# A prologue with its own step table: how the first groups of a graph-network kernel are started

## The chip, the cores and the metric

The kernel runs on one core of one Trainium2 chip. The metric is the device time of one execution in microseconds (us). The program is one instruction stream per engine (TensorE, written PE; VectorE, DVE; ScalarE, ACT; GpSimd, POOL) and the queue of SyncE (SP), which issues DMAs. Times inside an execution are counted from the start of its span.

## The reference

There are 128 independent graphs of 128 nodes with 256 features, and a weighted adjacency matrix for each. Two layers follow one another, all in float32:

```
h = relu(layernorm(x));  x1 = x + adj @ (h @ W0) + b0
h2 = relu(layernorm(x1))
p_h = h2 @ fc_w[:, head h] + fc_b        # 8 heads of 256
logits_h[n, m] = (p_h q_w)[n] + (p_h k_w)[m] + (1 - adj[n, m]) * (-1e9)
attn_h = softmax(leaky_relu(logits_h, 0.01))
out = x1 + sigmoid(concat_h(attn_h @ p_h) @ fp_w + fp_b + h2)
```

## The kernel before, in words

Work is done in 32 groups of 4 graphs. `s0`, `s1`, `s2`, ... are the groups; group g goes through several phases, and the main loop for group g also carries earlier phases of the groups g+1 to g+4. A pair is two graphs of a group, and a unit is one pair with four of its eight heads, so that a group has 4 units.

The weights of a head are folded: `setup_weights` (L208) multiplies a head's fc_w with its part of fp_w, so that the large product per head is attn @ h2 (`aggregate`, L562, tile g_ps) and then times the folded weights (`multiply`, L600, tile acc). Each 2x2 block product is done with seven products in place of eight; `take` (L573) forms their left sides f0 to f6 from g_ps on ACT, DVE and POOL, `setup_sums` (L272) forms the sums of weights, and `combine` (L618) puts the products together.

The vector that gives q and k is folded as well: `setup_wqk` (L184) makes fc_w times q_w and k_w, one product of two columns per head and half, into wqk_p. `setup_bias` makes the constant part. `setup_fb` (L244) and `setup_fb2` (L251) form fc_b times fp_w: twelve of sixteen chunks one after the other on DVE, four on POOL; `setup_fpb` (L260) sums over partitions on PE.

For a group the attention runs as: `make_qk` (L449) and `turn_qk` (L464) produce q and k; k is written to DRAM (k_mem) and read back spread over partitions by `load_k` (tile kq). `masked` (L495) spreads k with a DVE transpose and adds the mask; `leaky` (L508), eight ACT instructions for a graph; `head_max` (L516) on DVE; `exps` (L524), eight ACT instructions with sums; `normal` (L532) divides on POOL after a DVE reciprocal. The attention must then be transposed. `move` (L540) does it with 16 DMAs of 32-row blocks for a pair on the SP queue, and `turn` (L551) with a DVE transpose inside the blocks for each graph. The normalised h2 of the next groups is transposed in the same manner by `move_h2` (16 DMAs) and `turn_h2_blocks`, and in the prologue by `turn_h2` (PE transposes and ACT copies). `turn_blocks` and `turn_adj` are the same two ways for the adjacency.

The order on every engine is written by hand: under `manual_schedule` each engine executes the instructions in the order in which the program issues them, and waits at its head for what its instruction needs. A straight prologue prepares s0 and s1 and part of s2. Then the loop goes through the groups, each in 44 slots (four units of 11 entries); a slot has one PE step, and the table PLAN attaches other steps to it (slot, which group, function). For the first group a table FIRST_PLAN adds the steps which would otherwise belong to an earlier group, and the steps in `LATE` are left out of PLAN. All PSUM tiles but acc come from one pool of six.

```
    ORDER = [("g", 0, 0), 3, 0, ("g", 1, 1), 1, 4, ("g", 1, 0), 6, 5, ("g", 0, 1), 2]
    ps_m = ctx.enter_context(tc.tile_pool(name="ps_m", bufs=6, space=PSUM))
            if g == 0:
                for at_, f, *args in FIRST_PLAN:
            for at_, who, f, *args in PLAN:
                if at_ != slot or (g == 0 and f in LATE):
```

Of the kernel before, what the change touches and what calls it, by code (L numbers as in the profile page):

```python
# [9 lines left out]
FP = mybir.dt.float32  # L10
# [5 lines left out]
P = 128  # L16
D = 256
NC = D // P
H = 8
# [9 lines left out]
def gnn_then_gat_kernel(  # L29
# [109 lines left out]
    mk = sp.tile([P, 1], FP, name="mk")  # L139
    ones = sp.tile([P, P], FP, name="ones")  # L140
# [6 lines left out]
    def setup_rows():  # L147
# [3 lines left out]
        nc.vector.tensor_copy(cols, cp)  # L151
        for two in range(2):
# [31 lines left out]
    def setup_wqk(c):  # L184

        qk_cols = cols[:, NK:ROWS].rearrange("p (two c) -> p c two", two=2)
        wp = ps_m.tile([P, H, 2], FP, name="wp", tag="m")
        for h in range(H):
            for kk in range(NC):
                nc.tensor.matmul(  # L190
                    wp[:, h, :],
                    lhsT=fcwT[:, NC * h + kk, ts(c, P)],
                    rhs=qk_cols[:, kk, :],
                    start=(kk == 0),
                    stop=(kk == NC - 1),
                )
        nc.vector.tensor_copy(
            wqk_p[:, c, 0 : 2 * H].rearrange("p (two h) -> p two h", two=2),
            wp.rearrange("p h two -> p two h"),
        )  # L200

    def setup_wqk_order():
        for j in range(NB):
            for c in range(NC):
                n = 2 * (j % 2) + c
                nc.vector.tensor_copy(wqk[ts(j, Q), c], wqk_p[ts(n, Q), j // 2])
# [31 lines left out]


    NV = NK - 4  # L240
    fb = sp.tile([P, D], FP, name="fb")
    fb2 = sp.tile([P, NK - NV, D], FP, name="fb2")

    def setup_fb(k):  # L244
        col = cols[:, k : k + 1]
        if k == 0:
            nc.vector.tensor_scalar(fb, fpw[:, k], col, None, ALU.mult)
        else:
            nc.vector.scalar_tensor_tensor(fb, fpw[:, k], col, fb, ALU.mult, ALU.add)

    def setup_fb2():  # L251
        n = NK - NV
        nc.gpsimd.tensor_tensor(
            fb2, fpw[:, NV:NK], cols[:, NV:NK].unsqueeze(2).to_broadcast([P, n, D]), ALU.mult
        )
        while n > 1:
            n //= 2
            nc.gpsimd.tensor_tensor(fb2[:, 0:n], fb2[:, 0:n], fb2[:, n : 2 * n], ALU.add)
# [226 lines left out]

    def spread(s, b):

        if b % 2 == 0:
            s["a", b // 2] = at.tile([P, NB, 2, H, Q], FP, name="attn", tag="attn", bufs=3)
        nc.vector.transpose(  # L490
            s["a", b // 2][:, :, b % 2],
            s["kq"][:, :, b].unsqueeze(3).to_broadcast([P, NB, H, Q]),
        )

    def masked(s, b):  # L495
        spread(s, b)
        a = s["a", b // 2][:, :, b % 2]
# [10 lines left out]
    def leaky(s, b, h0=0, nh=H):  # L508
        a = s["a", b // 2][:, :, b % 2]
# [6 lines left out]
    def head_max(s, b):  # L516
        a = s["a", b // 2][:, :, b % 2]
# [6 lines left out]
    def exps(s, b, h0, nh):  # L524
        a = s["a", b // 2][:, :, b % 2]
# [6 lines left out]
    def normal(s, b):  # L532
        a = s["a", b // 2][:, :, b % 2]
# [6 lines left out]
    def move(s, pair, blocks=range(NB * NB), queues=(nc.sync,)):  # L540
# [4 lines left out]
        for n in blocks:  # L545
            i, j = divmod(n, NB)
            queues[n % len(queues)].dma_start(  # L547
                s["ab", pair][ts(j, Q), i], s["a", pair][ts(i, Q), j]
            )

    def turn(s, b):  # L551
# [4 lines left out]
        )  # L556

# [203 lines left out]
    LATE = (shift_both, n2_apply, move_h2, turn_h2_blocks, make_qk, turn_qk, load_k, turn)  # L761
# [39 lines left out]
    n2_apply(s0, 1)  # L801
    for half in range(2):
        n1_stats(s1, half)
    scale((s1, "n1"), root=True)
    setup_bias()
    begin(s2)
    setup_fb2()
    for k in range(NV):
        setup_fb(k)
    setup_wqk(0)  # L810
    turn_h2(s0, 0)
    turn_h2(s0, 1)
    setup_wqk(1)
    make_qk(s0, wqk_p)
    turn_qk(s0)
    load_k(s0)
    for half in range(2):
        n1_apply(s1, half)
    turn_adj(s1)
    make_mask(s1)  # L820
    add_b0(s1)
    for half in range(2):
        n1_stats(s2, half)
    first_a(s1, 0)
    first_a(s1, 1)
    masked(s0, 0)
    leaky(s0, 0)
    masked(s0, 1)
    leaky(s0, 1)
    first_b(s1, 0)  # L830
    first_b(s1, 1)
    head_max(s0, 0)
    exps(s0, 0, 0, H)
    head_max(s0, 1)
    exps(s0, 1, 0, H)
    setup_weights(0, 0, True)
    normal(s0, 0)
    n2_stats(s1, 0)
    setup_weights(0, 1, True)
    n2_stats(s1, 1)  # L840
    setup_weights(1, 0, True)
    scale((s1, "n2"), (s2, "n1"))
    normal(s0, 1)
    setup_weights(1, 1, True)
    for half in range(2):
        n2_apply(s1, half)
    for h in range(2, 4):
        setup_weights(h, 0, True)
        setup_weights(h, 1, True)
    turn_h2(s1, 0)  # L850
    turn_h2(s1, 1)
    move(s0, 0, queues=(nc.sync, nc.sync, nc.scalar))
    setup_weights(4, 0, True)
    setup_weights(4, 1, True)
    make_qk(s1, wqk_p)
    setup_wqk_order()
    masked(s0, 2)
    for h in range(5, H):
        setup_weights(h, 0, False)
        setup_weights(h, 1, False)  # L860
    leaky(s0, 2)
    masked(s0, 3)
    leaky(s0, 3)
    turn_qk(s1)
    load_k(s1)
    turn(s0, 0)
    turn(s0, 1)
    head_max(s0, 2)
    setup_fpb()
    setup_sums(0)  # L870
    exps(s0, 2, 0, H)
    setup.close()
    pool["un"] = ctx.enter_context(tc.tile_pool(name="unit", bufs=2))
    FIRST_PLAN = [
        (0, load_blocks, s2),
        (1, begin, s3),
        (1, turn_blocks, s2),
        (1, normal, s0, 2),
        (1, head_max, s0, 3),
        (1, n1_apply, s2, 0),  # L880
        (1, n1_apply, s2, 1),
        (2, exps, s0, 3, 0, H),
        (2, add_b0, s2),
        (6, normal, s0, 3),
        (6, move, s0, 1),
# [25 lines left out]
    for g in range(NG):  # L911
# [4 lines left out]
        for slot in range(4 * len(ORDER)):  # L916
# [6 lines left out]
            if g == 0:  # L923
                for at_, f, *args in FIRST_PLAN:
                    if at_ == slot:
                        f(*args)
# [53 lines left out]
```

## Time and profile before

| what | value |
|---|---|
| time, median of 3 runs | 1558.01 us (1555.54 to 1558.44) |
| profiled execution, its own time | 1552.82 us |
| span of that execution | 1550.9 us |
| PE busy | 1494.5 us (96%) |
| DVE busy | 1312.8 us (85%) |
| ACT busy | 1098.5 us (71%) |
| POOL busy | 938.3 us (61%) |
| mean granted TensorE clock | 0.982 |

A share of busy time is a mean over the whole span, and the stretch before the loop has other limits than the loop. The views by stretch, by waits and by time are therefore the ones to read. A line such as "L610 PE MATMUL acc<-wts,f" names a source line, the engine, the operation, the tile written and those read.

### The profile page before, as it was taken

How to read it: one execution, taken by the hardware profiler on the slowest of the kernel's cores; microseconds unless marked ns; L12 is line 12 of the kernel's file. 1: busy time of each engine (PE TensorE's matmuls, PEld its weight loads, DVE VectorE, ACT ScalarE, POOL GpSimd, SP SyncE). 2: the span in 40 equal slices, each digit the busy share in tenths (PEclk: the TensorE clock that was granted, in tenths of full speed). 3: DMA queues.
4: the chain of work that ended last, by engine and by line, in shares of the span. 5: the costliest groups of instructions: out<-in, count | busy, mean ns of one | idle time of the engine just before them, and what ended most of it. 6: DMA issues, size and time to landing. Idle time of an engine off the chain costs nothing.

```text
span 1550.9 us, 30658 instructions
## 1 busy us (share of the span) xinstructions
PE 1494.5 (96%) x9953; PEld 1209.9 (78%) x9953; DVE 1312.8 (85%) x2286; ACT 1098.5 (71%) x3830; POOL 938.3 (61%) x692
## 2 busy tenths in 40 slices
PE   7777999999999999999999999999999999999998
PEld 7655787888888878788878888877788887788786
DVE  5676888998888899888889988888998888898763
ACT  3683788767778867677877777787677778777651
POOL 3154665666666656676656667665566766566563
PEclk8889999999999999999999999999999999999999
DMA  5142444434444443444444344444434444433320
GB/s 184 31 90 64 92 96 96 97 81 104 106 91 99 95 95 83 101 107 85 98 96 98 83 103 100 93 99 96 94 85 104 98 96 97 97 79 82 74 69 27
DMA packets 259688, 142.07 MB, mean 92 GB/s; under 512 B 174900, under 2 KB 226504, under 8 KB 259272
## 3 DMA queue, kind: packets, MB, share of 16 engines
q1 hardware_dynamic: 259288, 139.79, 40.4%
q8 instruction: 78, 1.28, 0.4%
q14 instruction: 82, 0.67, 0.2%
q10 hardware_dynamic: 240, 0.33, 0.1%
HBM read 39.86 MB, written 17.30 MB: 37 GB/s over the span
## 4 chain that ended last, share of the span: by engine, by line
ACT 33%; DVE 31%; SPq 11%; PE 9%; issue 6%; DMA 6%; POOL 3%; DVEq 0%; ACTq 0%; POOLq 0%
ACT attn L527 14%; ACT attn L511 11%; SPq L547 9%; DVE attn L498 7%; DVE attn L490 5%; PE acc L610 4%; ACT h L320 4%; DMA attnB<-attn 4%; DVE st L286 4%; DVE attnT L554 3%; DVE f L586 2%; DVE x L391 2%; PE g_ps L565 2%; DVE f L587 2%; POOL attn L536 2%
## 5 line engine op out<-in xcount | busy, mean ns | idle before, releaser
L610 PEld LDWEIGHTS acc<-wts,f 128*128 128x128 f32 x7168 | 888.3, 192 | 260.4 <-issue 180.4
L610 PE MATMUL acc<-wts,f 128*128 128x128 f32 x7168 | 894.8, 275 | 15.7 <-DVE z L626 15.6
L565 PE MATMUL g_ps<-attnT,h 128*128 128x512 f32 x1024 | 530.6, 600 | 5.7 <-DVE attnT L554 3.8
L527 ACT ACTIVATE attn<-attn,nmax 128x128 f32<-128x128 f32 x1024 | 397.5, 397 | 0.0
L588 POOL TENSOR_TENSOR f<-f,f 128x512 f32<-128x512 f32 x128 | 163.4, 1277 | 356.3 <-DVE f L586 356.2
L511 ACT ACTIVATE attn<-attn,q 128x128 f32<-128x128 f32 x1024 | 313.0, 392 | 42.0 <-DVE attn L498 22.1
L536 POOL TENSOR_TENSOR attn<-attn,total 128x1024 f32<-128x1024 f32 x128 | 245.3, 1916 | 113.1 <-DVE total L535 98.7
L590 ACT COPY f<-g_ps 128x512 f32<-128x512 f32 x128 | 73.8, 576 | 267.6 <-PE g_ps L565 267.6
L591 POOL TENSOR_TENSOR f<-f,f 128x512 f32<-128x512 f32 x128 | 209.3, 1635 | 7.8 <-ACT f L590 5.2
L527 ACT ACTIVATION_READ_ACCUMULATOR attn<-attn,nmax 128x1 f32 x1024 | 201.3, 197 | 0.0
L498 DVE TENSOR_TENSOR attn<-attn,mask 128x1024 f32<-128x1024 f32 x128 | 186.4, 1456 | 4.5
L519 DVE TENSOR_REDUCE nmax<-attn 128x8 f32<-128x1024 f32 x128 | 153.9, 1203 | 23.4 <-ACT attn L511 23.3
L490 DVE STREAM_TRANSPOSE attn<-kq 128x1024 f32<-128x1024 f32 x128 | 157.1, 1228 | 14.8 <-DMA kq<-k_mem 14.8
L565 PEld LDWEIGHTS g_ps<-attnT,h 128*128 128x128 f32 x1024 | 156.6, 193 | 14.0 <-issue 9.8
L554 DVE STREAM_TRANSPOSE attnT<-attnB 128x1024 f32<-128x1024 f32 x128 | 153.1, 1215 | 9.7 <-DMA attnB<-attn 6.2
L586 DVE TENSOR_TENSOR f<-g_ps,f 128x512 f32<-128x512 f32 x128 | 87.0, 680 | 50.8 <-issue 24.5
L384 PE MATMUL x_ps<-w_sb,ahT 128*128 128x256 f32 x512 | 122.5, 383 | 0.0
L654 POOL TENSOR_TENSOR z<-z,h 128x256 f32<-128x256 f32 x128 | 90.7, 730 | 40.5 <-DVE z L626 39.9
L384 PEld LDWEIGHTS x_ps<-w_sb,ahT 128*128 128x128 f32 x512 | 94.1, 193 | 11.4 <-issue 0.5
L582 ACT COPY f<-g_ps 128x512 f32<-128x512 f32 x128 | 74.4, 581 | 40.2 <-PE g_ps L565 40.2
L664 DVE SCALAR_TENSOR_TENSOR z<-z,x 128x1024 f32<-128x1024 f32 (+1 forms) x33 | 90.1, 2730 | 7.9 <-ACT z L660 7.9
L587 DVE TENSOR_TENSOR f<-f,g_ps 128x512 f32<-128x512 f32 x128 | 86.4, 675 | 0.0
(93 smaller groups left out, 1282.3 us busy)
## 6 DMA issues: line engine op xcount, KB each, us to landing
attnB<-attn SPq DMA_DIRECT2D x1019, 64.0 KB, 2.0
xg<-in_x_dram SPq DMA_DIRECT2D x32, 512.0 KB, 4.0
out_dram<-z SPq DMA_DIRECT2D x31, 512.0 KB, 3.1
h2B<-h SPq DMA_DIRECT2D x480, 32.0 KB, 1.9
ag<-in_adj_dram SPq DMA_DIRECT2D x32, 256.0 KB, 4.5
agB<-in_adj_dram SPq DMA_DIRECT2D x120, 64.0 KB, 4.4
fcw<-in_L_gnn_fc_w_dram SPq DMA_DIRECT2D x2, 1024.0 KB, 6.8
fpw<-in_L_gnn_fp_w_dram SPq DMA_DIRECT2D x1, 2048.0 KB, 14.0
```

The source lines that it names most:

```text
L384: nc.tensor.matmul(op[:, bb, :], lhsT=s["ahT"][:, 2 * b2 + bb, c, :], rhs=w0_sb[:, c, :], start=(c == 0), stop=(c == NC - 1),)
L490: nc.vector.transpose(s["a", b // 2][:, :, b % 2], s["kq"][:, :, b].unsqueeze(3).to_broadcast([P, NB, H, Q]),)
L498: nc.vector.tensor_tensor(a, a, s["mask"][:, b, :] .rearrange("p (j c) -> p j c", c=Q) .unsqueeze(2) .to_broadcast([P, NB, H, Q]), ALU.add,)
L511: nc.scalar.activation(a[:, :, h, :], a[:, :, h, :], AF.Prelu, bias=s["q"][:, b, h : h + 1], alpha=0.01,)
L519: nc.vector.tensor_reduce(nmax, a.rearrange("p j h c -> p h j c"), AX.XY, ALU.max, negate=True)
L527: nc.scalar.activation(a[:, :, h, :], a[:, :, h, :], AF.Exp, bias=s["nmax", b][:, h : h + 1], accum_out=s["total", b][:, h : h + 1],)
L536: nc.gpsimd.tensor_tensor(a, a, total.unsqueeze(1).unsqueeze(3).to_broadcast([P, NB, H, Q]), ALU.mult)
L554: nc.vector.transpose(aT.rearrange("p h (i r) -> p i h r", r=Q), s["ab", b // 2][:, :, b % 2])
L565: nc.tensor.matmul(u["g", b, c], lhsT=s["h2"][:, 2 * pair + b].rearrange("p j c q -> p (j c q)")[:, ts(c, P)], rhs=s["aT", 2 * pair + b][: ...
L588: nc.gpsimd.tensor_tensor(new(5), f[4], f[0], ALU.subtract)
L591: nc.gpsimd.tensor_tensor(new(2), f[1], f[5], ALU.subtract)
L610: nc.tensor.matmul(acc[:, slot, :], lhsT=u["f"][m][:, h, :], rhs=wt[m][:, half * HU + h, :], start=(half == 0 and h == 0 and m in FIRST), ...
```

## The change

`setup_wqk` is turned round: the small q and k columns, padded to 32, are now the stationary side and fc_w the moving one, with 16 products of 256 columns into four strips of partitions, a copy, and four PE transposes (`setup_wqk_turn`). fc_b times fp_w is wholly on POOL, in two halves of eight chunks. For group 0 the attention tile is laid out head by head (`view`), and the transposed attention of s0 is made by PE transposes and copies on ACT and DVE (`turn_by_products`), without `move` and `turn`. The prologue's order is rewritten: statistics, copies of folded weights (the first four on ACT, most others on DVE) and the sums of weights stand in other places; `masked` of s1 and the wait for its `kq` come in the loop as before. The first period of the loop uses a full FIRST_PLAN in place of PLAN: in it s2's adjacency and h2 are transposed by PE, and `make_qk`, `turn_qk` and `load_k` of s2 stand in slots 32 to 34 (before: 38 to 40), ahead of the moves of s1's second pair (slot 40). From group 1 on PLAN is the same.

```diff
-    def setup_wqk(c):
-        qk_cols = cols[:, NK:ROWS].rearrange("p (two c) -> p c two", two=2)
-        wp = ps_m.tile([P, H, 2], FP, name="wp", tag="m")
-        for h in range(H):
-            for kk in range(NC):
-                nc.tensor.matmul(wp[:, h, :], lhsT=fcwT[:, NC * h + kk, ts(c, P)],
-                    rhs=qk_cols[:, kk, :],
...
+    def setup_wqk():
+        wp = ps_m.tile([P, 2, D], FP, name="wp", tag="m")
+        for n in range(2):
+            for g in range(4):
+                for kk in range(NC):
+                    nc.tensor.matmul(wp[ts(g, Q), n, :], lhsT=qkc[:, kk, :],
+                        rhs=fcwT[:, NC * (4 * n + g) + kk, :],
...
+        nc.vector.tensor_copy(wqk_rows, wp)
+    def setup_wqk_turn():
+        tp = ps_m.tile([P, 2, NC, P], FP, name="wt_ps", tag="m")
+        for n in range(2):
+            for c in range(NC):
+                nc.tensor.transpose(tp[:, n, c, :], wqk_rows[:, n, ts(c, P)], ident)
...
-    NV = NK - 4
-    def setup_fb(k):
...
+    def setup_fb():
+        for half in range(2):
+            n = NK // 2
+            ks = ts(half, n)
+            nc.gpsimd.tensor_tensor(
+                fb2, fpw[:, ks], cols[:, ks].unsqueeze(2).to_broadcast([P, n, D]), ALU.mult
+            )
+            while n > 1:
+                n //= 2
+                to = fb.unsqueeze(1) if n == 1 and half == 0 else fb2[:, 0:n]
+                nc.gpsimd.tensor_tensor(to, fb2[:, 0:n], fb2[:, n : 2 * n], ALU.add)
...
+    def turn_by_products(s, b):
+        aT = s["aT", b] = pool["attnT"].tile([P, H, P], FP, name="attnT", tag="attnT")
+        for h4 in range(2):
+            tp = ps_m.tile([P, 4, P], FP, name="aT_ps", tag="m")
+            for h in range(4):
+                n = H * (b % 2) + 4 * h4 + h
+                nc.tensor.transpose(tp[:, h, :], s["a", b // 2][:, ts(n, P)], ident)
+            copy = nc.vector.tensor_copy if h4 else nc.scalar.copy
+            copy(aT[:, ts(h4, 4)], tp)
...
+    FIRST_PLAN = [
...
+        (3, 0, exps, 2, 0, H),
+        (3, 0, head_max, 3),
...
+        (9, 0, normal, 2),
+        (9, 0, exps, 3, 0, H),
...
+        (12, 2, turn_adj),
+        (14, 1, masked, 0),
...
+        (16, 0, turn_by_products, 2),
+        (17, 1, leaky, 0),
+        (18, 0, turn_by_products, 3),
...
+        (25, 1, head_max, 1),
+        (25, 1, normal, 0),
+        (25, 2, shift_both),
+        (26, 2, n2_apply, 0),
...
+        (28, 2, turn_h2, 0),
+        (28, 1, normal, 1),
+        (28, 1, move, 0),
...
+        (32, 2, make_qk, wqk_p),
...
+        (34, 2, turn_qk),
+        (34, 2, load_k),
...
+        (37, 3, first_a, 0),
+        (37, 1, exps, 3, 0, H),
+        (38, 1, turn, 0),
+        (39, 1, turn, 1),
+        (39, 1, normal, 3),
+        (40, 1, move, 1),
...
     n2_apply(s0, 0)
     n2_apply(s0, 1)
+    setup_fb()
     for half in range(2):
         n1_stats(s1, half)
+    setup_wqk()
+    turn_h2(s0, 0)
+    turn_h2(s0, 1)
     scale((s1, "n1"), root=True)
+    setup_wqk_turn()
     setup_bias()
     begin(s2)
...
+    rdev((s1, "n2"), (s2, "n1"))
...
     normal(s0, 1)
+    shift((s1, "n2"), (s2, "n1"))
...
+    turn_by_products(s0, 0)
     turn_h2(s1, 0)
     turn_h2(s1, 1)
-    move(s0, 0, queues=(nc.sync, nc.sync, nc.scalar))
+    turn_by_products(s0, 1)
...
```

## The prediction

> **What bounds the kernel now.** I read the page first (busy shares and slices), then the table of windows for the stretches in which PE is not full, then who PE waited for, and last the order of time around each gap.
>
> ```profile
> PE 1494.5 (96%) x9953; PEld 1209.9 (78%) x9953; DVE 1312.8 (85%) x2286; ACT 1098.5 (71%) x3830; POOL 938.3 (61%) x692
> PEclk8889999999999999999999999999999999999999
> 25.00:50.00 25.00, 23.85 (x118) 22.05 (x119) 18.42 (x42) 8.92 (x23) 3.25 (x3) 0.60 0.03 5
> 50.00:75.00 25.00, 17.09 (x85) 13.11 (x83) 16.20 (x43) 16.46 (x58) 6.74 (x4) 0.86 0.19 43
> 75.00:100.00 25.00, 18.70 (x78) 13.29 (x79) 21.44 (x32) 24.57 (x95) 13.10 (x9) 0.80 0.32 74
> 150.00:175.00 25.00, 18.73 (x122) 15.19 (x123) 20.65 (x33) 24.49 (x97) 13.37 (x10) 0.80 0.41 80
> 175.00:200.00 25.00, 25.00 (x166) 20.76 (x165) 23.10 (x43) 12.88 (x33) 15.79 (x12) 1.00 0.39 93
> 300.00:700.00 400.00, 396.56 (x2691) 320.93 (x2690) 356.84 (x617) 296.69 (x1038) 258.26 (x185) 1.00 0.44 97
> ```
>
> Columns of the windows: length, then busy us of PE, PEld, DVE, ACT, POOL, then granted clock. From 175 us on PE is full at clock 1.00: the loop is bound by PE, whose order from group 1 on the change leaves alone. What can be won lies before 175 us, in idle PE and in a half-speed clock (0.60 from 25 to 50 us).
>
> ```profile
> PE acc L610 <- DVE z L626: 10.3, 1, 10.3
> PE ah_ps L368 <- DVE total L535: 6.1, 1, 6.1
> 75.23 3.28 PE L565 MATMUL g_ps<-attnT,h 128*128 128x512 f32 x4 [1.90 <-ACT attn L511]
> 156.27 3.75 PE L610 MATMUL acc<-wts,f 128*128 128x128 f32 x16 [10.31 <-DVE z L626]
> 109.81 10.33 SPq L427 DMA_DIRECT2D h2B<-h  x16
> 120.25 21.54 SPq L547 DMA_DIRECT2D attnB<-attn  x32
> 141.89 0.53 SPq L474 DMA_DIRECT2D k_mem<-k  x1
> 143.53 1.73 SPq L479 DMA_DIRECT2D kq<-k_mem  x4
> ```
>
> The loop starts at 75.23. Group 1's slot 0 is at 135.18, then PE stops for 10.31 us at slot 12. The wait names DVE's combine, but DVE itself stood 10.35 us for kq of s2 (it starts L490 at 146.62), and kq was queued on SP behind 48 block DMAs of 0.65 us. In the steady loop the 29 qk products of groups 1 to 29 lie from 170.22 to 1439.1: 1268.9/28 = 45.3 us a period; slot 0 to the qk of slot 24 takes 22.5 us. So group 1 really counts from 170.22 - 22.5 = **147.7**. The end moves by as much as this point does.
>
> **The change part by part.** Durations are those of the rows of this execution, start to start where instructions queue: masked 2.4 us, head_max 1.13, take's two DVE adds 1.2, stats of a group 2.1; leaky 2.37, exps 3.08, copy 0.47 to 0.59, apply of a group 2.0; normal 1.9, a POOL add of 512 columns 1.25, power (L302) 1.65; on PE a multiply 0.89, an aggregate 0.86, ah 1.8, x 3.5, a transpose 0.11 (0.24 at half clock).
>
> 1. *fc_b times fp_w on POOL.* Removed from DVE: L247 and eleven L249 (27.4 to 35.4). Added: two chains on POOL. The rows give 1.89 us for 4 chunks (1024 columns), so 3.8 for 8; adds of 1024, 512, 256: 2.4 (L338), 1.27, 0.73. A chain is 8.2, both 16.4, from 21.1 (fpw lands) to 37.5. The sum is wanted only by fb_ps (72.3) and POOL had 3.25 us of work from 25 to 50, so the length itself is hidden. What it blocks is not:
>
> ```profile
> 21.10 1.89 POOL L253 TENSOR_TENSOR fb<-fpw,cols 128x1024 f32<-128x1024 f32 x1 [8.27 <-DMA fpw<-in_L_gnn_fp_w_dram]
> 21.86 1.15 DVE L309 SCALAR_TENSOR_TENSOR nb<-mv,rstd 128x4 f32<-128x4 f32 x1
> L249 DVE SCALAR_TENSOR_TENSOR fb<-fpw,cols,fb x11: 483/485/2455, 27.8 to 33.0; 128x256 f32<-128x256 f32 x11
> ```
>
> nb has four columns and a median of 0.149; here it ends at 23.01, when POOL's product does, and one L249 grew by 2.0 us under a POOL add. The Trainium skill (SBUF — State Buffer, SBUF: two separate sides) says that a DVE instruction with two SBUF inputs and a POOL instruction exclude each other for the whole of the one that started first. By the rows alone nb would again be late by 1.1 us, k of s0 would leave at about 34; by the rule it waits for an instruction twice as long (to 24.9), and again for s1's nb (33.1) and qk_bias (35.5). I take the rule, since the row fits it to 0.02 us.
>
> 2. *wqk.* Removed: 64 narrow instructions on a half clock, 4.5 + 6.8 us of PE up to 36.6. Added: 32 instructions of 256 columns in four strips, 4 transposes, three copies. No row has this form. Serial at x_ps' 0.22 us it is 7 us, 14 at half clock; the four-strip qk_ps runs 16 in 0.66 where a full multiply takes 1.95, a third, so 2.4 or 4.7. I take about 5, the qk_ps form being nearest.
>
> 3. *The walk to k of s0.* nb 25.0; h2 25.1 to 27.2 on ACT (before 23.1 to 25.2); wp done 29.6; h2T 31.5, copied by 32.1; root, nb of s1 33.3; wqk_p 33.6; qk_bias 35.7; q_ps 36.5; k_mem issued at **36.8** against 39.19, 2.4 us earlier. kq takes 4.65 us (39.19 to 43.84): masked(0) at 41.5. leaky ends 49.2 (51.3), exps(0), (1) 56.6 (58.7). The four weight copies on ACT lie in the wait for kq.
>
> 4. *Between.* normal(0) 53.6 to 55.5, power to 57.2, and now the reciprocal of graph 1 stands ahead of nb: normal(1) starts at 57.2 and nb, queued on DVE, waits for it to 59.1. h2 of s1 59.4 to 61.4 (60.9 to 62.9). Behind it: turned attention and h2T (PE cold, to 63.9), leaky(2) 64.0 to 66.4, qk of s1 65.6, masked(3) to 69.3, last weights and fb_ps 68.8. **Slot 0 at 69.0**, 6.2 earlier. Removed on the way: 16 move DMAs and DVE's two turns (2.4 us); added: 16 transposes, two ACT and two DVE copies.
>
> 5. *The first period.* PE's own work is 16 aggregates 13.8, 21 multiplies 18.7, ah and x for two groups 10.6, transposes 3.2, qk 0.7: 47 us, so 116 if nothing stalled. ACT has leaky(3) to 71.7, then 6 exps, 4 leaky, 3 applies and 20 copies, about 45 us: it is nearly as full, and its order decides. Walked in order: exps(2) 72.6 to 75.7, exps(3) to 79.2 (before 88.7); POOL forms f5, f2, then normal(2) to 79.8, where PE waits 1.5; x of s2 ends 93.0; stats, power to 97.7; normal(0) of s1 is ready then and holds nb to 99.6, the same pattern; h2 of s2 99.8 to 101.8, PE idle 3.6. ACT without a break: exps(1) 104.9, h2T copies, leaky(2), h of s3, exps(2) 114.4, leaky(3), copies of ah 118.0, for which x of s3 waits 3.1. Then 7.0 us of PE: **group 1 slot 0 at 124.8**. Stalls 1.5 + 3.6 + 3.1 and under a us of others.
>
> 6. *SP.* Removed: 32 moves for s0, 16 h2 moves and 4 agB for s2. Moves of s1's pair 0 wait for normal(1), 107 to 117.3 (16 x 0.64); k_mem and kq behind them, landed at 122.5, with no further block DMA in front. Behind kq wait pair 1's moves: exps(3) 121.3, normal 123.4, moves to 133.6, and h2 of s3 to 144. turn(0) at 120.5 and turn(1) at 124.5 make slots 0 and 3. masked of s2 starts at 126.4, behind late x sums on DVE, 1.6 us after slot 0 (in group 2 it is level): combine ends 135.9 where PE's slot 12 comes at 135.3. I charge 1 us. The 10.3 us stall and its cold clock are gone.
>
> 7. *Costed at nothing:* the head-by-head layout (L498 reads blocks of 32 already at its 1.23; between -0.05 and +0.1 us on each of some 100 instructions, and mostly beside PE), the wait on old buffers of the setup pool, n1_stats and weight sums (DVE idle for kq, or 1.3 us inside step 4). If that cover is gone, 2 us.
>
> Sum: 147.7 - 124.8 - 1 = 21.9. I keep 21.5: 1552.8 - 21.5 = 1531.3 for a like profiled execution; it lay 5.2 below the median of the runs, so **1536.5**.
>
> **The rivals.**
> - *PE nearly unbroken.* nb slips in ahead of normal at 57.2 and 97.7 (2 us each), and ACT's copies of ah come in time (3.1). For it: DVE got its turn at 23.01 in 0.02 us. Against: nb is freed by POOL's own power, and POOL's next instruction is ready. Gain 29: 1529.
> - *ACT bounds the first period.* ACT was busy 24.57 of 25 us from 75 to 100 before; each late release hands on, slot 0 of group 1 falls to about 134, only the SP stall is won: gain 12.5, 1545.5.
> - *Slower: SP holds kq anyway.* k_mem of s2 stands behind 16 moves that wait for normal(1) of s1. If that normal came after 130 rather than at 107, kq would land past 145.5; with pair 1's moves and h2 behind it, group 1 would start later than now. Price: 1 us for each us past 130, say +4: 1562. It needs POOL or ACT to be 23 us later than walked; against it ACT's whole first period has 4.5 us of idle.
> - *It does not do what it says:* the slow clock could stay through the new wqk as through the old. It is in the sum already (half clock to 41); warm would give at most 1 us, since POOL's chain sets 35.5.
>
> **How the numbers follow.** The forecast 0.60, ACT-bound 0.20, nearly unbroken 0.14, no change 0.02, slower 0.04. The unknown costs (2 us each for the two blocked nb, 3 for ACT's order, 2 for step 7, some 3 of scatter of the runs) and both winning rivals give 1527 to 1549. About 0.2% (3.1 us) is what a measurement can tell from no change: faster 0.94, same 0.02, slower 0.04.
>
> **What would show it.** Right: k_mem of s0 at about 37, nb at 24.9 and 59 with durations near 2 to 3 us, first g_ps at 69, the second group's at 124 to 126, no 10 us wait for L626, PE full from there. Wrong: nb not lengthened; a PE wait over 5 us in the first period; kq of s2 landing after 130; the qk of group 1's slot 24 at other than 147 to 149; a loop period other than 45.3.

## The result and the profile after

| | before | after |
|---|---|---|
| median of the runs | 1556.78 us (1552.88 to 1558.44, 4 runs) | 1533.04 us (1530.25 to 1538.2, 4 runs) |
| profiled execution: own time, span | 1552.82, 1550.9 us | 1530.25, 1528.5 us |
| k_mem of s0 issued | 39.19 | 29.73 |
| first g_ps | 75.23 | 63.26 |
| slot 0 of group 1 | 135.18 | 121.22 |
| qk of slot 24 in group 1 | 170.22 | 147.55 |
| from there to the end of the span | 1380.7 us | 1381.0 us |

The ratio is 0.9855, with an interval of 0.9822 to 0.9888. The last two rows say where the gain lies: all of it (22.7 us of a span 22.4 us shorter) is there at slot 24 of group 1, and the loop behind it is as it was.

The page of the changed kernel, its shares and its clock by slices, and the table of windows of the same kernel (length, busy us of PE, PEld, DVE, ACT, POOL, granted clock, DMA):

```profile
PE 1481.2 (97%) x9969; PEld 1195.8 (78%) x9969; DVE 1312.9 (86%) x2275; ACT 1101.8 (72%) x3836; POOL 954.4 (62%) x698
PEclk9999999999999999999999999999999999999999
25.00:50.00 25.00, 19.66 (x111) 15.74 (x112) 20.09 (x42) 16.47 (x54) 17.63 (x10) 1.00 0.13 36
50.00:75.00 25.00, 19.50 (x109) 13.56 (x107) 20.80 (x32) 19.54 (x73) 14.04 (x10) 0.93 0.09 14
75.00:100.00 25.00, 20.74 (x127) 16.78 (x128) 19.36 (x37) 17.92 (x58) 13.17 (x9) 0.96 0.13 33
150.00:175.00 25.00, 25.00 (x166) 20.71 (x165) 22.39 (x42) 11.91 (x33) 19.71 (x14) 1.00 0.46 99
300.00:700.00 400.00, 397.45 (x2692) 320.78 (x2691) 357.92 (x618) 301.16 (x1064) 254.87 (x185) 1.00 0.43 96
```

The slow clock of the first stretches is gone (1.00 where it was 0.60, 0.96 where it was 0.80), although PE is still idle for 4.3 to 5.5 us in each of the first three. The three views below, with only the lines that matter here, are what PE waited for in the first 180 us (total, times, longest), PE's timeline, and SP's queue in the first period:

```profile
PE h2T_ps L452 <- ACT h L330: 5.9, 2, 3.1
PE aT_ps L585 <- POOL attn L555: 2.9, 1, 2.9
```

```profile
63.26 4.45 PE L596 MATMUL g_ps<-attnT,h 128*128 128x512 f32 x10
96.97 2.17 PE L452 MATMUL h2T_ps<-ident,h 128*128 128x128 f32 x8 [3.06 <-ACT h L330]
121.22 1.02 PE L596 MATMUL g_ps<-attnT,h 128*128 128x512 f32 x2
133.01 2.02 PE L641 MATMUL acc<-wts,f 128*128 128x128 f32 x16 [1.08 <-DVE z L657]
147.55 0.67 PE L464 MATMUL qk_ps<-h2T,wqk 128*32 128x128 f32 x16 [2.83 <-DVE h2T L441]
```

```profile
103.73 10.11 SPq L566 DMA_DIRECT2D attnB<-attn  x16
113.93 0.53 SPq L484 DMA_DIRECT2D k_mem<-k  x1
115.58 1.75 SPq L489 DMA_DIRECT2D kq<-k_mem  x4
123.02 10.33 SPq L566 DMA_DIRECT2D attnB<-attn  x16
133.45 11.48 SPq L437 DMA_DIRECT2D h2B<-h  x16
```

The stop of 10.31 us at the combine is down to 1.08 us, since kq of s2 is issued at 115.58 instead of 143.53, with one set of 16 block DMAs ahead of it in place of three. A new wait of 2.83 us stands at slot 24: h2 of s3 goes through 16 block DMAs that are queued until 144.9, and the qk product needs their turned copy.

The walk to k of s0 ended 7 us before the predicted 36.8. The timeline of DVE and POOL in the changed kernel:

```profile
21.16 0.16 DVE L319 SCALAR_TENSOR_TENSOR nb<-mv,rstd 128x4 f32<-128x4 f32 x1
21.22 3.60 POOL L262 TENSOR_TENSOR fb<-fpw,cols 128x2048 f32<-128x2048 f32 x1 [8.36 <-DMA fpw<-in_L_gnn_fp_w_dram]
```

nb began 0.06 us ahead of POOL's product, and so did not wait for it. What that chance is worth is the subject of the first experiments.

### The profile page after: what moved, and what is told of

Same layout as the page of the kernel before. It is cut to its first block, busy times and chain, and to the rows that moved or that the text cites. A ratio compares the mean times of both kernels' runs of the same rounds, so it can differ in the third digit from the quotient of the medians.

```text
span 1528.5 us, 30616 instructions
## 1 busy us (share of the span) xinstructions
PE 1481.2 (97%) x9969; PEld 1195.8 (78%) x9969; DVE 1312.9 (86%) x2275; ACT 1101.8 (72%) x3836; POOL 954.4 (62%) x698
## 4 chain that ended last, share of the span: by engine, by line
ACT 32%; DVE 30%; SPq 11%; PE 9%; issue 6%; DMA 6%; POOL 4%; DVEq 0%; ACTq 0%; POOLq 0%
ACT attn L546 13%; ACT attn L530 11%; SPq L566 8%; DVE attn L517 7%; PE acc L641 5%; DVE attn L509 5%; ACT h L330 4%; DVE st L296 3%; DMA attnB<-attn 3%; DVE attnT L574 3%; PE g_ps L596 3%; SPq L437 2%; POOL attn L555 2%; DVE f L617 2%; DVE x L401 2%
## 5 line engine op out<-in xcount | busy, mean ns | idle before, releaser
L517 DVE TENSOR_TENSOR attn<-attn,mask 128x1024 f32<-128x1024 f32 x128 | 190.3, 1487 | 4.5
L574 DVE STREAM_TRANSPOSE attnT<-attnB 128x1024 f32<-128x1024 f32 x124 | 148.5, 1216 | 8.6 <-DMA attnB<-attn 5.9
L617 DVE TENSOR_TENSOR f<-g_ps,f 128x512 f32<-128x512 f32 x128 | 87.0, 680 | 48.0 <-issue 26.3
```

The lines of the kernel that those rows point to most:

```text
L517: nc.vector.tensor_tensor(a, a, s["mask"][:, b, :] .rearrange("p (j c) -> p j c", c=Q) .unsqueeze(2) .to_broadcast([P, NB, H, Q]), ALU.add,)
L574: nc.vector.transpose(aT.rearrange("p h (i r) -> p i h r", r=Q), s["ab", b // 2][:, :, b % 2])
```

## The experiments

c1, e1, e2, e3 were timed together (before: 1554.23 us), e4 to e7 (1555.01), and c2, e8, e9, e10 (1557.22). The table gives the medians; the other columns are from the one profiled execution of each, in us from the start of its span.

| kernel | median | ratio, 95% | nb of s0: start, length | k_mem s0 | first g_ps | slot 24 |
|---|---|---|---|---|---|---|
| after (first set) | 1533.04 | 0.9855 [0.9822, 0.9888] | 21.16, 0.16 | 29.73 | 63.26 | 147.55 |
| c1, after again | 1534.29 | 0.9866 [0.9848, 0.9885] | 21.74, 0.16 | 30.40 | 62.78 | 148.83 |
| c2, after again | 1539.09 | 0.9889 [0.9872, 0.9906] | 22.06, 3.44 | 37.45 | 68.99 | 154.44 |
| e1 fb on DVE | 1542.99 | 0.9921 [0.9895, 0.9948] | 21.87, 1.79 | 39.96 | 71.93 | 158.18 |
| e2 old wqk | 1539.53 | 0.9905 [0.9885, 0.9924] | 20.39, 0.16 | 39.31 | 70.20 | 155.69 |
| e3 nb late | 1538.43 | 0.9893 [0.9873, 0.9912] | 22.66, 2.54 | 37.15 | 68.49 | 153.78 |
| e4 moves for s0 | 1544.41 | 0.9924 [0.9907, 0.9941] | 20.45, 0.16 | 30.40 | 67.03 | 160.42 |
| e5 before, early k of s2 | 1546.64 | 0.9936 [0.9917, 0.9956] | 20.67, 0.16 | 38.07 | 75.05 | 165.35 |
| e6 shift first | 1532.25 | 0.9842 [0.9823, 0.9860] | 20.63, 0.16 | 29.80 | 60.57 | 145.43 |
| e7 kq behind moves | 1549.29 | 0.9961 [0.9944, 0.9979] | 22.05, 3.36 | 37.37 | 69.01 | 167.27 |
| e8 nb late, pieces | 1537.53 | 0.9870 [0.9855, 0.9885] | 23.10, 0.67 | 32.60 | 64.83 | 149.05 |
| e9 shift first, h2 by PE | 1529.47 | 0.9816 [0.9802, 0.9829] | 21.17, 0.16 | 30.42 | 61.22 | 143.91 |
| e10 all four | 1529.54 | 0.9819 [0.9805, 0.9832] | 21.05, 0.16 | 29.00 | 60.91 | 143.71 |

**c1 and c2: the changed kernel again.**

> The changed kernel itself once more, as the standard for the three kernels beside it. If the end moves with the point at which the loop becomes full, the qk product of group 1's slot 24 is at 147.5 us as before, and span minus that point is 1381 us. If nb of s0 got ahead of the POOL product of fc_b and fp_w at 21.2 us only by luck, this run can show it late: nb near 24.9, k_mem near 36, span some us longer. If nb's place is firm, it is at 21.2 again.

> The changed kernel once more, as the standard of this set, with five rounds. So far nb of s0 got ahead of the POOL product in two profiles of the changed kernel (21.2, 21.7) and in one of a kernel with the same prologue it did not (22.1, ended 25.4). Theory: the two cases differ by 4 to 6 us at the end, so that runs of one and the same kernel spread from 1530 to 1539. Rival: the spread has another origin, and it is as wide in kernels whose nb is not at risk.

The profiled execution of c2 had the other order. Its DVE and POOL rows:

```profile
22.06 3.44 DVE L319 SCALAR_TENSOR_TENSOR nb<-mv,rstd 128x4 f32<-128x4 f32 x1
21.87 3.60 POOL L262 TENSOR_TENSOR fb<-fpw,cols 128x2048 f32<-128x2048 f32 x1 [8.63 <-DMA fpw<-in_L_gnn_fp_w_dram]
```

Here nb, an instruction of 0.16 us, came 0.19 us after POOL's product and lasted until 25.50, where the product ends (25.47). k of s0 left at 37.45, the first g_ps was at 68.99, slot 24 at 154.44, 6.9 us later than in the first profile. It is one kernel with two outcomes. In c1 nb was 0.15 us ahead (21.74 against 21.89), in e7 0.25 us behind. POOL's start is set by the landing of fp_w, nb's by DVE's statistics, and neither is tied to the other.

Not all of the distance between the two profiles is nb's. Their spans differ by 11.7 us: 6.9 up to slot 24 and 4.8 behind it, so the theory and the rival of the second expectation each have a part. The order of nb in the untraced runs is not known. In each of the three sets the runs with the higher mean granted clock are the faster ones (0.997 for 1530.25 us to 0.989 for 1538.2 in the first), which fits both, since a late nb also leaves PE idle long enough for the clock to fall: in c2 it is 0.50 from 25 to 31 us.

**e3: nb made late on purpose**, by computing one half's statistics twice (the same values): two more pairs of short DVE instructions ahead of it.

```
     for half in range(2):
         n2_stats(s0, half)
+    n2_stats(s0, 1)
     scale((s0, "n2"), root=True)
```

> One of the two n2 statistics steps of s0 is done twice on DVE (1.06 us), so that nb of s0 is asked for at about 22.2 us, after POOL has begun the 128x2048 product at 21.2. Theory (a DVE instruction with two SBUF inputs waits for the whole POOL instruction): nb ends at 24.9 and not at 22.4, h2 of s0 follows, nb of s1 and qk_bias get behind the second product (33.1) and its first addition (35.5), k_mem at 34 to 37, first g_ps 3 to 6 us later than 63.3, span longer by 2 to 6 us. Rival (nb was never in danger, POOL yields): nb at 22.4, everything 1.1 us later, span longer by at most 1.1 us.

DVE's timeline in e3, and POOL's first product there:

```profile
22.66 2.54 DVE L319 SCALAR_TENSOR_TENSOR nb<-mv,rstd 128x4 f32<-128x4 f32 x1
32.22 1.25 DVE L319 SCALAR_TENSOR_TENSOR nb<-mv,rstd 128x4 f32<-128x4 f32 x1
33.79 2.11 DVE L252 SCALAR_TENSOR_TENSOR qk_bias<-mk,qkb,both 128x1 f32<-128x1 f32 x1
21.58 3.60 POOL L262 TENSOR_TENSOR fb<-fpw,cols 128x2048 f32<-128x2048 f32 x1 [8.69 <-DMA fpw<-in_L_gnn_fp_w_dram]
```

All three instructions end when POOL's of that moment does, as the predicted walk had it (24.9, 33.1 and 35.5 there; 25.20, 33.47 and 35.90 here; the two products end at 25.18 and 33.45). It is not every DVE instruction that waits: in the first profile the statistics, which read one tile, ran under POOL's first product from 22.44 on in their usual 0.39 to 0.41 us each. k left at 37.15, slot 24 was 6.2 us later than in the first profile, and the median is 4.1 us above that of c1 beside it.

**e8: e3 with POOL's product and adds cut into pieces of 512 columns**, so that a blocked DVE instruction gets its turn sooner.

```
-            nc.gpsimd.tensor_tensor(
-                fb2, fpw[:, ks], cols[:, ks].unsqueeze(2).to_broadcast([P, n, D]), ALU.mult
-            )
+            for q4 in range(4):
+                qs = ts(q4, 2)
+                k2 = ts(4 * half + q4, 2)
+                nc.gpsimd.tensor_tensor(
+                    fb2[:, qs], fpw[:, k2], cols[:, k2].unsqueeze(2).to_broadcast([P, 2, D]), ALU.mult
+                )
...
-                nc.gpsimd.tensor_tensor(to, fb2[:, 0:n], fb2[:, n : 2 * n], ALU.add)
+                for i0 in range(0, n, 2):
+                    i1 = min(i0 + 2, n)
+                    nc.gpsimd.tensor_tensor(
+                        to[:, i0:i1], fb2[:, i0:i1], fb2[:, n + i0 : n + i1], ALU.add
+                    )
```

> The kernel with the doubled statistics step (nb of s0 asked for behind the start of the POOL product), and now the products of fc_b and fp_w and their additions on POOL in pieces of at most 512 columns, about 1 us each, in place of 128x2048. Theory (a blocked DVE instruction waits for the one POOL instruction that is running): nb lasts at most 1.1 us in place of 2.5, the later waits shrink likewise, k_mem at 33 to 35 in place of 37.2, the mask additions lose under 1 us each; span 1.5 to 4 us shorter than the 1535.7 of the unpieced one. Rival (POOL's queue as a whole holds the port, or the pieces' own overhead makes the chain much longer): nb as late, k_mem not under 36.5.

nb lasted 0.67 instead of 2.54 us, k left at 32.60 instead of 37.15, and slot 24 came 4.7 us earlier than in e3. The mechanism is shown as far as that point. The end, expected 1.5 to 4 us earlier, isn't: the stretch after slot 24 took 1387.0 us in this execution and 1381.9 in e3 (PE was idle for 21.2 us of it against 17.2), and the intervals of the two medians overlap.

**e1: fc_b times fp_w on DVE again** (twelve chunks there, four on POOL, at the place after begin(s2)).

```
-    setup_fb()
...
     begin(s2)
+    setup_fb2()
+    for k in range(NV):
+        setup_fb(k)
```

> Undoes one part of the change: fc_b times fp_w again in twelve steps on DVE and four chunks on POOL, at the old place on DVE ahead of qk. Theory (POOL has room, DVE has not): DVE gets 7.7 us of work ahead of qk, saves 2.2 us of waits of nb and qk_bias behind POOL and 2.4 us of the two mask additions: k_mem goes from 29.7 to 34 or 35, the first g_ps from 63.3 to about 65, span longer by 1 to 3 us. Rival (the long POOL chain is a net loss, because DVE's two-input instructions wait for it): k_mem within 2 us of 29.7, first g_ps earlier than 63, span shorter by 1 to 3 us.

DVE's and PE's timeline in e1:

```profile
31.02 7.89 DVE L264 SCALAR_TENSOR_TENSOR fb<-fpw,cols,fb 128x256 f32<-128x256 f32 x11
39.23 0.47 PE L483 MATMUL q_ps<-ident,qk 128*128 128x128 f32 x1 [7.56 <-DVE qk L477]
```

The eleven sums stand between qk_bias and the copy of qk, and PE waits 7.56 us for that copy. k left at 39.96. Undoing this part alone costs 8.7 us against c1, where 1 to 3 were expected: one of the eleven took 2.45 us while POOL added for 2.34, nb was late in this execution (1.79 us) and early in c1's, and the clock was 0.78 from 20 to 40 us (1.00 in the first profile). So the 8.7 us are not the chain's alone. What part 1 brings is the removal of this chain from DVE, and not a faster product.

**e2: the old wqk**, 64 PE instructions of two columns.

```
-    setup_wqk()
+    setup_wqk(0)
+    setup_wqk(1)
...
-    setup_wqk_turn()
```

> Undoes another part: wqk by 64 narrow instructions of two columns, everything else changed. Theory (the narrow products keep the clock low and PE long): granted clock 0.5 from about 24.6 to past 35, the products take 11 us in place of 2.5, k_mem at 36 to 38 in place of 29.7, weights and ah of s1 at half speed behind, first g_ps at 67 to 70, span longer by 3 to 6 us. Rival (the clock fell before because PE had little to do, whatever the form, or the prologue is bound by DVE and POOL): clock falls only later or not at all, k_mem within 3 us of 29.7, span within 2 us.

PE's timeline and the window from 20 to 40 us, first of e2, then of the changed kernel:

```profile
20.67 13.08 PE L196 MATMUL wp<-cols,fcwT 128*128 128x2 f32 x64 [1.97 <-ACT fcwT L185]
20.00:40.00 20.00, 19.11 (x100) 18.13 (x101) 6.68 (x24) 6.99 (x15) 16.40 (x9) 0.54 0.21 49
```

```profile
21.44 2.48 PE L197 MATMUL wp<-fcwT,qkc 128*32 128x256 f32 x32 [1.97 <-ACT fcwT L185]
20.00:40.00 20.00, 16.61 (x127) 14.07 (x128) 15.32 (x37) 11.71 (x28) 18.23 (x9) 1.00 0.23 51
```

The old form takes 13.08 us where the new takes 2.48, and PE is counted busy for 19.11 of 20 us at a granted clock of 0.54. The clock was still 1.00 when the 64 narrow instructions began; it fell to 0.50 at 21.5 us, 0.8 us into them, and they did not bring it up again. The 32 wide ones, after the same wait of 1.97 us, ran at 1.00. Whether the narrow form or the wait before it started the fall is not shown. In c2, where nb was late, the clock fell under the wide form too: its last 24 instructions took 3.64 us, and it was back at 1.00 by 32 us. e2 costs 5.2 us against c1, with nb early in both profiles.

**e4: the attention of s0 by moves and turns again**, with the tile's layout as in the kernel before.

```
-        (16, 0, turn_by_products, 2),
-        (18, 0, turn_by_products, 3),
+        (16, 0, move, 1),
+        (20, 0, turn, 2),
+        (20, 0, turn, 3),
...
-    turn_by_products(s0, 0)
-    turn_by_products(s0, 1)
+    move(s0, 0, queues=(nc.sync, nc.sync, nc.scalar))
+    turn(s0, 0)
+    turn(s0, 1)
```

> Undoes one part of the change: the attention of s0 is transposed by 16 block DMAs a pair and DVE again (layout as in the other groups), everything else changed. Theory (the DMA way is too slow where PE waits for it): pair 0 leaves at 54.7, its 16 DMAs take 7 us on two queues and land by 64, turns on DVE 66 to 68, first g_ps about 67; pair 1's moves run from 79 to 89, turn to 94, and unit 2's first g_ps, at 84.2 in the changed kernel, waits to about 93: span longer by 6 to 10 us. Rival (PE transposes and copies cost ACT and DVE as much as they save): span within 2 us.

PE's and SP's timeline in e4:

```profile
94.88 2.05 PE L593 MATMUL g_ps<-attnT,h 128*128 128x512 f32 x2 [9.44 <-DVE attnT L571]
81.95 10.02 SPq L563 DMA_DIRECT2D attnB<-attn  x16
```

The 16 moves of the second pair are issued from 81.95 to 91.97, and PE waits 9.44 us for their turn; another 4.06 us stand ahead of the first g_ps. Sixteen transposes on PE instead cost 1.09 us for each eight at full clock. This part is worth about 10 us in the changed kernel (1544.41, against 0.9866 x 1555.01 = 1534.2).

**e7: kq of s2 behind the moves of s1's second pair.** Only load_k is moved.

```
         (34, 2, turn_qk),
-        (34, 2, load_k),
...
         (40, 1, move, 1),
+        (40, 2, load_k),
```

> The changed kernel, with only the four k loads of s2 put behind the 16 moves of s1's second pair on SP (slot 40 after move). Theory (what the order on SP is worth): these moves end at 133.4, kq lands near 137, masked of s2 starts there and not at 123.0, combine of the last units reaches 145, and PE stops at slot 12 for 10 to 13 us in place of 1.1: span longer by 9 to 13 us. Rival (late x sums on DVE set masked, kq has room): span longer by less than 4 us.

SP's and PE's timeline in e7:

```profile
130.45 10.32 SPq L566 DMA_DIRECT2D attnB<-attn  x16
140.81 2.03 SPq L489 DMA_DIRECT2D kq<-k_mem  x4
153.75 3.75 PE L641 MATMUL acc<-wts,f 128*128 128x128 f32 x16 [14.40 <-DVE z L657]
```

With one DMA step in another place PE stops for 14.40 us at the combine. c2 is the execution to set beside it (nb late in both): slot 24 at 167.27 against 154.44. This is the slower rival built on purpose; its price is real, but the change doesn't have that order.

**e5: the part alone, on the kernel before:** h2 of s2 by PE transposes, and make_qk, turn_qk and load_k ahead of the moves.

```
-        (16, move_h2, s2),
-        (34, turn_h2_blocks, s2),
-        (38, make_qk, s2),
-        (40, turn_qk, s2),
-        (40, load_k, s2),
+        (24, turn_h2, s2, 0),
+        (24, turn_h2, s2, 1),
+        (28, make_qk, s2, wqk_p),
+        (30, turn_qk, s2),
+        (30, load_k, s2),
```

> One part alone on the kernel before: in the first period h2 of s2 is transposed by PE (slot 24), and qk, its transpose and the k loads stand in slots 28 to 30, ahead of the moves of s1's second pair; nothing else. Theory (the 10.3 us stop in group 1 is kq behind the block DMAs): kq of s2 lands some 15 us earlier than at 146.5, the stop at 156 goes, group 1's slot 24 at 158 to 161 in place of 170.2, span shorter by 9 to 12 us, about half of the change's gain; the other half is the prologue and the first period. Rival (the combine on DVE is late for other reasons): a stop of 5 us or more stays, span shorter by at most 5.

PE's timeline in e5:

```profile
118.03 1.55 PE L454 MATMUL qk_ps<-h2T,wqk_p 128*32 128x128 f32 x16 [2.69 <-ACT h2T L447]
141.53 1.10 PE L565 MATMUL g_ps<-attnT,h 128*128 128x512 f32 x2 [0.87 <-DVE attnT L554]
153.17 2.02 PE L610 MATMUL acc<-wts,f 128*128 128x128 f32 x16 [0.86 <-DVE z L626]
```

The stop of 10.31 us is gone (0.86), but slot 24 came only 4.9 us earlier in this execution, and the median 8.4 us. Slot 0 of group 1 went from 135.18 to 141.53: the transposes, copies and a new wait of 2.69 us fill a first period that is otherwise still the old one. My expectation missed in size, since it counted the stop and not what the early steps take in a full period.

**e6: shift ahead of normal**, so that nb isn't queued behind POOL's division, in the prologue and in the first period.

```
-        (25, 1, normal, 0),
         (25, 2, shift_both),
+        (25, 1, normal, 0),
...
-    normal(s0, 1)
     shift((s1, "n2"), (s2, "n1"))
+    normal(s0, 1)
```

> The changed kernel with two swaps on DVE: the shift (nb) that follows the power on POOL stands ahead of the reciprocal that lets the next normal start, for s1 in the prologue and for s2 in slot 25. Theory (nb waits 1.9 us for that normal each time): nb 0.2 us each, at 52.9 and 94.5; h2 of s1 and of s2 1.6 us earlier each, first g_ps about 62, the wait of PE for h2 of s2 3.1 to about 1.5; group 1's slot 24 at 144 to 146 in place of 147.5, span shorter by 2 to 3 us. Rival (normal is as urgent as nb, its delay of half a us to 2 us costs the same): span within 1 us, with PE waiting for normal or for moves in place of h2.

DVE's timeline, first of the changed kernel, then of e6:

```profile
52.81 1.93 DVE L319 SCALAR_TENSOR_TENSOR nb<-mv,rstd 128x4 f32<-128x4 f32 x2 [0.58 <-POOL rstd L312]
94.42 1.94 DVE L319 SCALAR_TENSOR_TENSOR nb<-mv,rstd 128x4 f32<-128x4 f32 x2 [0.54 <-POOL rstd L312]
```

```profile
52.89 0.23 DVE L319 SCALAR_TENSOR_TENSOR nb<-mv,rstd 128x4 f32<-128x4 f32 x2 [1.58 <-POOL rstd L312]
93.24 0.23 DVE L319 SCALAR_TENSOR_TENSOR nb<-mv,rstd 128x4 f32<-128x4 f32 x2 [0.65 <-POOL rstd L312]
```

A swap of two lines takes 1.7 us from each pair, and the first g_ps is at 60.57. But the median is only 1532.25, and the qk after that of slot 24, a period later, was at 193.35 where the changed kernel had it at 192.72. PE's timeline and its windows, first of e6, then of the changed kernel, tell why:

```profile
145.43 1.11 PE L464 MATMUL qk_ps<-h2T,wqk 128*32 128x128 f32 x16 [3.05 <-DVE h2T L441]
149.00:150.00 1.00, 1.00 (x6) 1.00 (x6) 0.00 (x0) 1.00 (x6) 1.00 (x2) 0.50 0.53 94
```

```profile
149.00:151.00 2.00, 2.00 (x18) 1.88 (x17) 0.04 (x1) 2.00 (x10) 2.00 (x3) 1.00 1.22 175
```

The wait for the h2 block DMAs is still there (3.05 us), and this time the clock went down with it: 0.50 from 145 to 151 us and 0.67 in the next, so 3.1 us of work lost while PE was busy. What was won ahead of slot 24 was given back there.

Part of it had been lost before. The qk of s2 came 4.4 us earlier than in the changed kernel (99.47 against 103.84), slot 24 only 2.1. In between PE waits 2.50 us for adjT, which it does not in the changed kernel, and adjT stands on DVE behind z. DVE's and POOL's timeline in e6:

```profile
104.50 2.75 DVE L657 TENSOR_TENSOR z<-w,v 128x256 f32<-128x256 f32 x2
104.42 2.35 POOL L348 TENSOR_TENSOR xg<-xg,b_bc 128x1024 f32<-128x1024 f32 x1 [0.64 <-ACT h L330]
```

Here z comes 0.08 us behind POOL's addition and lasts until 107.25, beyond the addition's end at 106.77. In the changed kernel the two z instructions began 0.44 us ahead of the addition (106.86 against 107.30) and took 0.62 us together. Both engines are earlier in e6, POOL by half a us more: the swap freed nb and made another two-input instruction late.

**e9: e6, and h2 of s3 transposed on PE in group 1**, without its 16 DMAs.

```
+                if g == 1 and f == turn_h2_blocks:
+                    turn_h2(s3, 0)
+                    turn_h2(s3, 1)
+                    continue
```

(move_h2 is skipped and make_qk takes wqk_p in that group.)

> The kernel with nb ahead of normal in both places, and in group 1 h2 of s3 transposed by PE and copied by ACT in place of 16 block DMAs and a DVE transpose. Theory (the 2 us won by the swap were lost at group 1's slot 24, where PE waited 3.05 us for the block DMAs of h2 and then ran at half clock): that wait goes, clock stays 1.00 from 140 on, the qk of slot 24 at 143 to 144 and, two groups on, no later than 190.5; 0.9 us more PE work; span 2 to 4 us under the changed kernel. Rival (another wait takes its place, on the moves of s1's second pair or on ACT): slot 24 not before 145.5, span within 1 us of the swapped kernel's 1531.0.

PE's timeline in e9, then the second qk in the changed kernel:

```profile
143.91 0.67 PE L464 MATMUL qk_ps<-h2T,wqk_p 128*32 128x128 f32 x16
189.79 0.67 PE L464 MATMUL qk_ps<-h2T,wqk 128*32 128x128 f32 x16 [0.19 <-DVE h2T L441]
```

```profile
192.72 0.67 PE L464 MATMUL qk_ps<-h2T,wqk 128*32 128x128 f32 x16 [0.19 <-DVE h2T L441]
```

No wait is left at slot 24, which comes 3.6 us earlier than in the first profile, and a period later the kernel is 2.9 us ahead. The median is 1529.47 us: its four runs (1526.54 to 1530.33) lie below all five of c2 beside it (1536.87 to 1545.22), and its interval of ratios (0.9802 to 0.9829) below those of c1 and c2, and only 0.0007 into that of the first set. That e9 beats the changed kernel by as much as its set says (9.6 us) is not shown: nb of s0 was late in c2's profile and early in e9's, and its order in the other runs is not known. With nb early in both, what is shown is the 3.6 us at slot 24. The profiled span is the same 1528.5 as that of the first profile, because the loop behind took 3.6 us longer in that execution.

This scatter of the loop (1380.7 to 1387.0 us from slot 24 to the end over all profiles here) can be traced in part. Near its end every one of the fourteen profiles has a stop of PE at the combine of 2.5 to 2.9 us. The table of windows shows it, first of the changed kernel (2.67 us idle, clock 1.00), then of e6 (2.90 us idle, clock 0.91):

```profile
1440.00:1460.00 20.00, 17.33 (x112) 13.45 (x111) 19.27 (x26) 19.32 (x76) 8.09 (x7) 1.00 0.16 46
```

```profile
1440.00:1460.00 20.00, 17.10 (x99) 13.43 (x99) 18.96 (x26) 16.92 (x65) 7.21 (x7) 0.91 0.18 51
```

The clock stays at 1.00 behind it in three profiles (before, the first one and c1) and falls to 0.50 for some 3 to 4 us in the other eleven. Behind slot 24 it fell in c2, e1, e4 and e6. The work lost to the clock from slot 24 on is 0 in the three, whose loops took 1380.7 to 1381.0 us, and 1.5 to 4.8 us in the others. If that and PE's idle time (17.0 to 21.2 us) are taken off, all fourteen lie between 1362.5 and 1364.0 us.

**e10: e9, the pieces of e8, and two steps earlier in the tables.**

```
         (7, "u", take, 0, 1, 0),
+        (7, 0, normal, 2),
         (9, "u", take, 0, 0, 1),
-        (9, 0, normal, 2),
...
+        (28, 3, turn_blocks),
...
-        (34, 3, turn_blocks),
```

> A version meant to beat the changed kernel: the two swaps of nb; h2 of s3 by PE; the POOL products and additions in pieces of 512 columns; normal of s0's graph 2 one POOL instruction earlier (slot 7, ahead of f2); adjacency of s3 turned in slot 28 and not 34. Theory (each wait seen in the trace is worth its length, about 1.5, 2, 1, 2 and 2 us, less what overlaps): qk of group 1's slot 24 at 139 to 142, span 5 to 8 us under the changed kernel, and less spread from run to run. Rival (ACT, without a break of work in the first period, hands each gain back): slot 24 not before 144, span at most 3 us shorter.

Slot 24 was at 143.71, where 139 to 142 was expected, and the median 1529.54: the further edits bring nothing measurable over e9. PE's wait of 2.55 us for adjT in e9 is gone, but z on DVE is late behind POOL as before (2.81 us), and PE waits 2.07 us for ahT in the same stretch. For aT it waits 2.06 + 0.52 us in place of 2.88. A wait that is shortened comes back at the next release.

## Why the prediction was right, and where it was not

The time was right: 1536.5 predicted, 1533.04 measured, and 22.4 us gained in the profiled span against a sum of 21.9. Its order of nb was off by 5.7 us one way, steps 5 and 6 together by 5.0 the other way, and in the first profile these nearly cancel. By the prediction's own list of signs that execution speaks on both sides: the qk of slot 24 is where it should be, but "nb not lengthened" stood among the signs of being wrong.

| step | predicted | first profile (nb ahead) | c2 (nb behind) |
|---|---|---|---|
| 3: k_mem of s0 | 36.8 | 29.73 | 37.45 |
| 4: first g_ps | 69.0 | 63.26 | 68.99 |
| 5: slot 0 to slot 0 | 55.8 | 58.0 | 59.6 |
| 6: slot 0 to slot 24 | 22.5 + 1 | 26.3 | 25.8 |
| slot 24 of group 1 | 147 to 149 | 147.55 | 154.44 |

- *Steps 1 and 3, the rule.* The prediction took the rule of the Trainium skill (SBUF — State Buffer, SBUF: two separate sides) against the single short row, and assumed that POOL always starts first. The rule held wherever POOL did: c2, e7 and e3 give 37.45, 37.37 and 37.15 for 36.8. The assumption on the order failed: the trace of before showed 0.76 us between POOL's start and nb's, and I read that as fixed. It is a distance between a DMA's landing and a chain on DVE, and runs of one kernel lie on both sides of zero. Worth 5.7 us at the first g_ps, with what the idle PE does to the clock.
- *Step 2.* The four-strip form by its nearest row (2.4 us warm) was exact: 2.48. In the first profile the clock was 1.00 instead of the assumed half. In c2, where PE waited another 2.75 us for a copy queued behind nb, the assumption held: the last 24 instructions took 3.64 us and ended at 29.79, for 29.6 predicted. The full multiply x_ps takes 3.62 us for 16 in the same profile, so the strips run at about a third of that each.
- *Step 4.* nb waits for normal: 1.9 predicted, 1.93 measured. What the rival "nearly unbroken" hoped for did not occur by itself; e6 made it so by order.
- *Step 5, mis-sized by 2.2 us.* Stalls of 1.5, 3.6 and 3.1 were predicted, and 2.88, 3.06 and 1.39 measured: the sum is nearly right. The first is longer because POOL's division, for which PE waits, was itself held by DVE (2.89 us for 1.91, shown below). PE's own work was taken as 47 us, and PE was busy for 50.34 of 57.96. After the wait of 3.06 us the granted clock was 0.59, 0.50, 0.50 and 0.70 in the four us from 98 to 102, which is 1.7 us of work lost; a wait was priced at its length, without what the clock adds. The other 1.6 us isn't taken apart.
- *Step 6.* The stop is gone as predicted, kq was issued at 115.58 and no block DMA stood between k_mem and it; the combine cost 1.08 for the 1 us charged. What failed is the term put at nothing: the list of the SP queue has "h2 of s3 to 144" and no charge for it, and PE waited 2.83 us at slot 24 for the turned copy of those DMAs, which were queued until 144.93.
- *The rivals.* ACT did not bound the first period (group 1 at 121.22, not 134). SP did not hold kq; e7 built that case, and it cost 12.8 us at slot 24 against c2. The changed wqk does not keep the slow clock in the first profile (1.00 from 20 to 40 us); with nb late, in c2, it was 0.50 from 25 to 31 us and from 35 to 41.
- *The luck in it.* In c2, where step 3 went as predicted, slot 24 was 6 us later than the sum said and the profiled execution took 1541.98, not 1531.3; the other 4.8 us lie in the loop behind, 3.2 of them work lost to the clock. The underestimates of steps 5 and 6 were paid for by an order of nb that the prediction had excluded. It was also luck that the two profiles compared, that of before and the first one, both lost nothing to the clock behind slot 24 (c2 did). Over the three sets the medians are 1533.04, 1534.29 and 1539.09.

The parts do not add up: undone singly in the changed kernel, they cost 8.7 us (e1, against c1), 5.2 (e2), about 10 (e4) and 12 to 15 (e7, against c2's ratio and c1's), 36 to 39 together, for a gain of some 20. Each undone part delays the same chain, and the clock goes with it: its mean was 0.986 to 0.988 in these four profiles and 0.997 in c1's. How much of each price is the clock's is not taken apart.

## What to carry to other kernels

Where two engines exclude each other, look at which of the two is ready first, by how much, and what sets each of the two times; if it is less than the scatter of a DMA's landing, put both outcomes into the range, or fix the order in the program as e6 did, and then look which other pair of instructions has changed its order. A wait of some 3 us on PE costs more than its length when the clock falls after it, so price it at once to twice its length (e6: 3.05 us, and 3.1 lost behind it). And every group of DMAs that a walk lists on a queue needs a line on who waits for its end.

## What the runs showed of the hardware

- An instruction of four columns took 3.44 us by coming 0.19 us late, or 0.16 by coming 0.06 us early, and with it came 7 us at slot 24; making it late by an edit (e3) gave 6.2.
- The exclusion works the other way as well. With a masked add on DVE from 72.29 to 74.27 (itself 1.98 us in place of 1.23, under POOL's addition before), POOL's division of 1.91 us, begun at 73.15, took 2.89. POOL's and DVE's timeline in the changed kernel:

```profile
52.74 1.91 POOL L555 TENSOR_TENSOR attn<-attn,total 128x1024 f32<-128x1024 f32 x1
73.15 2.89 POOL L555 TENSOR_TENSOR attn<-attn,total 128x1024 f32<-128x1024 f32 x1
72.29 1.98 DVE L517 TENSOR_TENSOR attn<-attn,mask 128x1024 f32<-128x1024 f32 x1
```

- The length of a wait does not say whether the clock falls. At slot 24 waits of 2.83 and 3.06 us left it at 1.00 (the first profile, c1), one of 1.93 us was followed by half clock for about 3 us (e4), one of 2.32 us likewise (c2), and one of 3.05 us by more than 6 us of it (e6). The Trainium skill (TensorE: Matmul & The Clock Gate, What's actually happening) gives an idle window of about 3.4 us, free-running, as what turns the clock down. A phase that differs by run would fit this scatter, though no run here shows the phase; that 1.93 and 2.32 us were enough does not fit the length, and the measurement decides.
- With products of two columns the clock was at half for 12 of 13 us, with PE counted as busy (e2).
